# Four copies on one engine, a shorter distance at the last tiles, and a fifth output buffer in a two-layer expert kernel

## The chip, the cores and the metric

The kernel runs on one core of a Trainium2 chip. A core has a matrix engine (TensorE, PE in the profile; its weight loads are the row PEld), a vector engine (VectorE, DVE), an engine for activation functions (ScalarE, ACT), a general one (GpSimd, POOL) and one that mostly issues DMAs (SyncE, SP). Each works through its own queue in order; they wait for each other by semaphores. The time is the device time of one execution in microseconds, lower is better.

## The reference

The input x is 8 sequences of 256 tokens with 128 features, 2048 tokens in all, in float32. Two layers follow, each a conditioning step and a mixture of 8 experts (128 to 512 and back to 128).

```python
x = x + L0_ffn(L0_cond(x, itok_2))      # layer 0
x = x + L1_ffn(L1_cond(x, itok_8))      # layer 1

# L0_cond: scores = tanh(x W1 + b1) v; softmax over a prefix, a postfix or all other tokens; pooled x / count
# L0_ffn: gates = logits * (logits >= the 3072nd smallest logit); every expert for every token
h = gelu_tanh(x @ w1[e].T + b1[e]);  y = h @ w2[e].T + b2[e];  out = sum_e gates[e] * y
# L1_cond: a small adapter by the sequence's language, then a layer norm with that language's gamma and beta
# L1_ffn: layer norm; the two best of 8 experts for each token, weighted
out = sum over the two best of w * (gelu(xn @ w1[e] + b1[e]) @ w2[e] + b2[e]);  return out + residual
```

## The kernel before

**Front.** The 2048 tokens are four groups of 512 (`NG = 4`), each a tile of 128 partitions with four tokens in each. For each group TensorE turns the tokens into PSUM (L224, tile xTp), and a copy brings them to SBUF as xT: for groups 0 and 2 on ScalarE (L229), for groups 1 and 3 on VectorE (L227). `products` (L203) multiplies a group's xT with the conditioning weights and the gate's weights; a few matmuls into a tile `idle` (L190) only keep TensorE running. VectorE then adds a bias row bv (L206; bv itself is copied out of PSUM at L233), ScalarE takes tanh (L207), VectorE multiplies and sums (L211, L212). The sums of all groups are turned at once (L248); two scans over them (L251, L253), two more operations (L255, L256) and the matmuls `top` (L262) lead to the softmax and the pooling. The counts cnt (L314, L315) are needed only behind the pooling.

**Layer 0, dense.** `layer` goes over five units of tokens (three of 512, two of 256) and over 8 experts in each: four matmuls of 512 columns to the hidden layer (L784), its activation on ScalarE (L786), and four matmuls back (L764), one expert later. Between them a function `pump` takes single steps of what else is to do: a search for the threshold of the gates, the pooling of later groups, and for a finished unit the adapter, the norm, the routing and the scatter of its tokens to a list in DRAM, sorted by expert (xs, L676, from GpSimd).

**Layer 1, sparse.** The list is worked on in tiles of 128 rows of one expert. The first `SURE = 36` tiles (0 to 35) are always there. A tile k has four steps. `fetch` loads its rows (L814) and its expert's first weights (L822) by SyncE's queue. `turn` transposes the rows (L829), scales them on VectorE (L831) and copies the expert's bias (L833). `hidden` is four matmuls (L840) and four activations (L842). `output` is four matmuls (L849) into one of two PSUM buffers yps, an add of the expert's second bias on VectorE into a tile yt (L852, four buffers), a scale by the token's weight on ScalarE (L853), and a scatter of the 128 rows to their places in DRAM from GpSimd (ys, L854). A buffer of yt is free again when the scatter that reads it has landed.

The steps of several tiles are interleaved by three queues of the program: `fetched`, `flipped` (turned) and `hid` (with a hidden layer). `proceed(ahead, between)` does one `hidden` if more than `ahead` tiles are turned, and one `output` if more than `ahead` have a hidden layer. `AHEAD = 2` keeps two tiles' distance between the steps of one tile. After tile 35 is turned, `proceed(0)` empties the queues.

**End.** All engines then read the number of tiles (L901) and branch (L903) over a body for tiles 36 to 38, which these inputs don't need. Where it is left out, each engine brings the semaphores that the body would have raised up to date. Then the rows ys are loaded back (L911, two queues, eight tiles), added to the residual (L914, L915) and stored (L916).

The order of instructions on each engine is not the order of the lines alone: a planner of the language sets it from the dependences and its own estimates, so the built order has to be looked at where a change is made.

Of the kernel before, what the change touches and what calls it, by code (L numbers as in the profile page):

```python
# [10 lines left out]
F32 = mybir.dt.float32  # L11
# [10 lines left out]
B, S, D = 8, 256, 128  # L22
P = 128
# [19 lines left out]
SURE = 36  # L43
# [8 lines left out]
AHEAD = 2  # L52
# [16 lines left out]
def tile_adaln_ffn_d2(ctx: ExitStack, tc: tile.TileContext, x, ptype, lang, cols, b1v,  # L69
                      w10, w20, w11d, w21d, lw1, lw2, lgb, out):  # L70
    nc = tc.nc
# [6 lines left out]
    work = ctx.enter_context(tc.tile_pool(name="work", bufs=2))  # L78
# [27 lines left out]
    for e in range(E):  # L106
        t = first.tile([P, HC * P], F32, tag="w1", name=f"w10_{e}")
        nc.sync.dma_start(out=t, in_=w10[e])
        w10s.append(t)
        t = const.tile([P, HC, D], F32, name=f"w20_{e}")  # L110
# [42 lines left out]
    for b in range(B):  # L153
        at = nc.values_load(lgi[0:1, b:b + 1], engines=(SP,), min_val=0, max_val=NL - 1,
                            skip_runtime_bounds_check_because="a language's number")
        for lst, name, src, rows, width in (
# [3 lines left out]
            t = const.tile([rows, width], F32, name=f"{name}_{b}")  # L160
# [10 lines left out]
    xT, poolT, resid, gd0 = {}, {}, {}, {}  # L171
# [26 lines left out]
    def products(g):  # L198

        space = (psy, "y") if g < 2 else (psb, "big")  # L200
        xa = space[0].tile([P, GT, A + E], F32, tag=space[1], name=f"xa{g}")
        for t in range(GT):
            nc.tensor.matmul(xa[:, t, :], lhsT=xT[g][:, t * P:(t + 1) * P], rhs=col[:, C_W1:C_W1 + A + E],  # L203
                             start=True, stop=True)
        pass_time(1, ident, xT[g][:, :S])
        nc.vector.tensor_tensor(at[:, g], xa[:, :, :A], bv[:, 0].unsqueeze(1).to_broadcast([P, GT, A]), ALU.add)  # L206
        nc.scalar.activation(at[:, g], at[:, g], AF.Tanh)  # L207
        nc.scalar.copy(xg[g][:, :, D:D + E], xa[:, :, A:])

    def scores(g):  # L210
        nc.vector.tensor_tensor(at[:, g], at[:, g], bv[:, 1].unsqueeze(1).to_broadcast([P, GT, A]), ALU.mult)  # L211
        nc.vector.tensor_reduce(sl[:, g * GT:(g + 1) * GT], at[:, g], AX.X, ALU.add)  # L212
# [8 lines left out]
    for g in range(NG):  # L221
        tp = psb.tile([P, GT, P], F32, tag="big", name=f"xTp{g}")
        for t in range(GT):
            nc.tensor.transpose(tp[:, t, :], xg[g][:, t, :D], ident)  # L224
        xT[g] = keep.tile([P, GN], F32, tag="xT", name=f"xT{g}")
        if g % 2:
            nc.vector.tensor_copy(xT[g], tp.rearrange("p t d -> p (t d)"))  # L227
        else:
            nc.scalar.copy(xT[g], tp.rearrange("p t d -> p (t d)"))  # L229
        if not g:  # L230
            nc.tensor.matmul(bvp.rearrange("p c a -> p (c a)"), lhsT=ones[:A, :],
                             rhs=diag.rearrange("k c a -> k (c a)"), start=True, stop=True)
            nc.vector.tensor_copy(bv, bvp)  # L233
        else:
            products(g - 1)
        if g > 1:
            scores(g - 2)
# [21 lines left out]
    for g in range(NG):  # L259
        tp = psb.tile([P, 2, S], F32, tag="big", name=f"top{g}")  # L260
# [458 lines left out]
    def pump():  # L719
        if gd0:  # L720
            n = next(ready)
            if not n:
                gates0.append(gd0[0])
            if waiting and n >= 0 and n % DRAIN == 0:
                waiting.popleft()()
        if behind:
            if next(behind[0], done) is done:
                behind.popleft()
# [72 lines left out]
    def expert(k, *engines):  # L801

        rows, i = lists[listing(k)], k - SLOTS.get(listing(k) - 1, 0)
        return nc.values_load(rows[0:1, 1, i:i + 1], engines=engines, min_val=0, max_val=E - 1,
                              skip_runtime_bounds_check_because="at most E - 1, a sum of flags")
# [21 lines left out]
    def turn(k, xt, wt):  # L827
        tp = pss.tile([P, P], F32, tag="sm", name=f"xtp{k}")
        nc.tensor.transpose(tp, xt[:, :D], ident)  # L829
        xc = work.tile([P, P], F32, tag="xc", name=f"xc{k}", bufs=AHEAD + 3)  # L830
        nc.vector.tensor_scalar(xc, tp, col[:, C_LG:C_LG + 1], col[:, C_LB:C_LB + 1], ALU.mult, ALU.add)  # L831
        b1 = small.tile([P, HC], F32, tag="b1", name=f"b1_{k}", bufs=AHEAD + 3)
        nc.vector.tensor_copy(b1, b1all[:, bass.ds(expert(k, DVE), 1), :].rearrange("p o c -> p (o c)"))  # L833
        return k, xt, wt, xc, b1

    def hidden(k, xt, wt, xc, b1):
        hp = psb.tile([P, HC, P], F32, tag="big", name=f"hps{k}")
        hT = work.tile([P, HC, P], F32, tag="scr", name=f"hs{k}", bufs=NSCR)
        for c in range(HC):
            nc.tensor.matmul(hp[:, c, :], lhsT=wt[:, c * P:(c + 1) * P], rhs=xc, start=True, stop=True)  # L840
        for c in range(HC):
            nc.scalar.activation(hT[:, c, :], hp[:, c, :], AF.Gelu, bias=b1[:, c:c + 1])  # L842
        return k, xt, hT

    def output(k, xt, hT):
        ek = expert(k, PE, DVE)
        yp = psy.tile([P, D], F32, tag="y", name=f"yps{k}")
        for c in range(HC):
            nc.tensor.matmul(yp, lhsT=hT[:, c, :], rhs=w21[:, bass.ds(ek, 1), c * D:(c + 1) * D],  # L849
                             start=(c == 0), stop=(c == HC - 1))  # L850
        yt = work.tile([P, D], F32, tag="yt", name=f"yt{k}", bufs=4)
        nc.vector.tensor_tensor(yt, yp, b2all[:, bass.ds(ek, 1), :].rearrange("p o d -> p (o d)"), ALU.add)  # L852
        nc.scalar.activation(yt, yt, AF.Copy, scale=xt[:, D + 1:D + 2])  # L853
        move = nc.gpsimd.indirect_dma_start(  # L854
            out=ys, out_offset=bass.IndirectOffsetOnAxis(ap=xt.bitcast(I32)[:, D:D + 1], axis=0),
            in_=yt, in_offset=None, bounds_check=2 * NT * P - 1, oob_is_err=False)
        tc.declare_no_dep(move.ins, group="outputs", reason="no two outputs share a row")
        tc.add_to_no_dep_group("outputs", move.ins)

    fetched, flipped, hid = deque(), deque(), deque()  # L860

    def proceed(ahead, between=lambda: None):
        if len(flipped) > ahead:
            hid.append(hidden(*flipped.popleft()))
        between()
        if len(hid) > ahead:
            output(*hid.popleft())

    def ahead(k):

        if k < SURE:
            finished(("first", listing(k)))
            fetched.append(fetch(k))
# [14 lines left out]
    for k in range(PRIMED, SURE):  # L888
        ahead(k + LEAD)
        if k == SLOTS[NU - 2]:  # L890

            while len(flipped) > 1 or len(hid) > 1:
                proceed(1)
        flipped.append(turn(*fetched.popleft()))
        pump()
        proceed(AHEAD, pump)
    while flipped or hid:
        proceed(0)
    while behind:
# [3 lines left out]
    with tc.If(more > SURE - SLOTS[NU - 2]):  # L903
        for k in range(SURE, NSLOT):
            output(*hidden(*turn(*fetch(k))))
# [61 lines left out]
```

## Time and profile before

| | us |
|---|---|
| three runs | 380.01, 388.47, 388.97 (median 388.47) |
| the profiled execution, and its span | 380.68, 379.0 |
| TensorE busy | 345.8 (91% of the span) |
| VectorE, ScalarE, GpSimd busy | 195.0, 167.0, 94.5 |
| mean clock granted to TensorE | 0.977 of full |
| first matmul of layer 0 | starts at 29.37 |
| add of tile 35 (L852) | starts at 361.64 |
| last scatter ys (L854) | starts at 362.64 |
| first reload yg (L911) | issued at 365.17 |

All rows from the third on come from the trace of the profiled execution; times within it count from the start of its span. A line of the page's groups names the line of the kernel, the engine, the operation, what is written and read, how often, and the busy time. In a timeline a row has its start, its duration, and in brackets how long the engine had been idle and what ended that. An engine's name with a q is its sequencer, which waits, branches and issues DMAs. The ends of matmuls are modelled.

### The profile page before, as it was taken

The numbers are of one execution on the slowest core, as the hardware profiler recorded it, in microseconds if no ns is written. First come the engines' busy times: TensorE is split into PE (matmuls) and PEld (weight loads), VectorE is DVE, ScalarE is ACT, GpSimd is POOL, SyncE is SP. The second block draws the span as 40 slices with busy tenths as digits, with TensorE's granted clock in tenths as the row PEclk, the third lists the DMA queues.
The fourth block names the chain that finished last, engine by engine and source line by source line (L and its number), as shares of the span: only waits on it lengthen the run. The fifth ranks groups of instructions, "written<-read, shape, count | busy, mean of one in ns | idle before, by whom it ended". The sixth has DMA issues, their size and how long they took to land. (4 is left out here: it accounts for less than half of the span.)

```text
span 379.0 us, 5911 instructions
## 1 busy us (share of the span) xinstructions
PE 345.8 (91%) x1596; PEld 233.0 (61%) x1596; DVE 195.0 (51%) x801; ACT 167.0 (44%) x387; POOL 94.5 (25%) x142
## 2 busy tenths in 40 slices
PE   6799999999999999999999999989989879999900
PEld 6695444444444445445445688857869769999900
DVE  4775565542245675565512474847576644333305
ACT  2166434553542244223443244425635637567800
POOL 8100000000000030650350021262045565444530
PEclk9999999999999999999999999999999998999975
DMA  6935999005222101210130001126543554566136
GB/s 189 382 84 150 368 379 356 4 0 148 69 77 102 56 30 55 63 49 30 56 69 14 28 29 42 36 65 175 151 121 107 162 162 121 168 187 173 47 117 244
DMA packets 33603, 46.12 MB, mean 122 GB/s; under 512 B 5349, under 2 KB 16375, under 8 KB 33569
## 3 DMA queue, kind: packets, MB, share of 16 engines
q1 hardware_dynamic: 29024, 39.26, 34.6%
q0 software_dynamic: 2304, 4.37, 3.2%
q10 hardware_dynamic: 2240, 2.10, 1.6%
q8 instruction: 14, 0.23, 0.3%
q14 instruction: 21, 0.16, 0.1%
HBM read 31.57 MB, written 14.39 MB: 121 GB/s over the span
## 5 line engine op out<-in xcount | busy, mean ns | idle before, releaser
L786 ACT ACTIVATE hT_first<-hp_first,col 128x512 f32<-128x512 f32 (+1 forms) x160 | 93.4, 601 | 103.3 <-PE hp_first L784 102.3
L784 PE MATMUL hp_first<-poolT,w 128*128 128x512 f32 (+1 forms) x320 | 121.2, 513 | 1.3 <-DVE xr L591 0.7
L764 PE MATMUL yp_first<-hT_first,w 128*128 128x512 f32 (+1 forms) x320 | 120.6, 511 | 0.0
L784 PEld LDWEIGHTS hp_first<-poolT,w 128*128 128x128 f32 x320 | 58.8, 190 | 44.2 <-issue 38.2
L764 PEld LDWEIGHTS yp_first<-hT_first,w 128*128 128x128 f32 x320 | 59.0, 190 | 42.5 <-issue 38.6
L676 POOL DMA_INDIRECT xs<-zr,pos x32 | 31.5, 986 | 64.3 <-DVE pos L674 27.9
L842 ACT ACTIVATE hs<-hps,b 128x128 f32<-128x128 f32 x144 | 40.6, 365 | 11.2 <-PE hps L840 5.3
L854 POOL DMA_INDIRECT ys<-yt,xt x36 | 35.2, 977 | 40.9 <-ACT hs L842 28.3
L849 PE MATMUL yps<-w,hs 128*128 x288 | 39.6, 283 | 2.5 <-DVE row L558 2.4
L840 PE MATMUL hps<-xc,wt 128*128 128x128 f32 x288 | 39.2, 280 | 1.1 <-issue 1.1
L849 PEld LDWEIGHTS yps<-w,hs 128*128 128x128 f32 x288 | 35.7, 195 | 4.3 <-issue 3.5
L752 DVE SCALAR_TENSOR_TENSOR part_first<-yp_first,col,gbc_first 128x512 f32<-128x512 f32 (+1 forms) x28 | 17.2, 614 | 40.4 <-PE yp_first L764 39.9
L840 PEld LDWEIGHTS hps<-xc,wt 128*128 128x128 f32 x288 | 36.0, 196 | 0.8 <-issue 0.6
L853 ACT ACTIVATE yt<-yt,xt 128x128 f32<-128x128 f32 x36 | 14.6, 405 | 23.3 <-issue 15.0
L754 DVE TENSOR_TENSOR acc_first<-acc_first,part_first 128x512 f32<-128x512 f32 (+1 forms) x35 | 20.1, 580 | 0.5
L579 POOL MEMSET ha<- 1x512 f32 x5 | 2.6, 516 | 67.6 <-PE dp L588 67.4
L406 POOL DMA_DIRECT2D gd_L<-gT_L x1 | 0.6, 649 | 74.3 <-DVE gT_L L404 74.3
L833 DVE COPY b<-col 128x4 f32 x36 | 7.2, 200 | 23.0 <-ACT hs L842 17.7
L852 DVE TENSOR_TENSOR yt<-yps,b2all 128x128 f32<-128x128 f32 x36 | 10.5, 291 | 14.8 <-PE yps L849 7.1
L831 DVE TENSOR_SCALAR xc<-xtp,col 128x128 f32<-128x128 f32 x36 | 14.4, 401 | 4.0 <-PE xtp L829 2.4
L772 ACT ACTIVATE y_first<-yp_first,col 128x512 f32<-128x512 f32 x8 | 5.5, 687 | 24.2 <-PE yp_first L764 24.2
L420 DVE TENSOR_SCALAR_CACHE_REDUCE fl<-logit,tr 128x128 f32<-128x128 f32 x46 | 13.5, 343 | 0.6
(205 smaller groups left out, 304.2 us busy)
## 6 DMA issues: line engine op xcount, KB each, us to landing
wt<-in_w_dram SPq DMA_DIRECT2D x36, 256.0 KB
xs<-empty SPq DMA_DIRECT2D x1, 8580.0 KB
w<-in_w_dram SPq DMA_DIRECT2D x24, 256.0 KB
gbc_first<-gd_L SPq DMA_DIRECT2D x24, 256.0 KB
xt<-xs SPq DMA_DIRECT2D x36, 65.0 KB
gbc_first<-gd_L SPq DMA_DIRECT2D x16, 128.0 KB
lgb<-in_lgb_dram SPq DMA_DIRECT2D x8, 128.0 KB
yg<-ys ACTq DMA_DIRECT2D x4, 256.0 KB
```

The source lines that it names most:

```text
L676: move = nc.gpsimd.indirect_dma_start(out=xs, out_offset=bass.IndirectOffsetOnAxis(ap=pos[:, t:t + 1], axis=0), in_=zr[s][:, t, :], in_off ...
L752: nc.vector.scalar_tensor_tensor(part, y, bias, gbc, ALU.add, ALU.mult)
L754: nc.vector.tensor_tensor(accs[u], accs[u], part, ALU.add)
L764: nc.tensor.matmul(yp, lhsT=w2s[e][:, c, :], rhs=hT[:, c, :], start=(c == 0), stop=(c == HC - 1))
L784: nc.tensor.matmul(hp, lhsT=w1s[e][:, c * P:(c + 1) * P], rhs=sources[g][:, o * P:o * P + n], start=True, stop=True)
L786: nc.scalar.activation(hT[:, c, :], hp, act, bias=col[:, cb1 + e * HC + c:cb1 + e * HC + c + 1])
L831: nc.vector.tensor_scalar(xc, tp, col[:, C_LG:C_LG + 1], col[:, C_LB:C_LB + 1], ALU.mult, ALU.add)
L840: nc.tensor.matmul(hp[:, c, :], lhsT=wt[:, c * P:(c + 1) * P], rhs=xc, start=True, stop=True)
L842: nc.scalar.activation(hT[:, c, :], hp[:, c, :], AF.Gelu, bias=b1[:, c:c + 1])
L849: nc.tensor.matmul(yp, lhsT=hT[:, c, :], rhs=w21[:, bass.ds(ek, 1), c * D:(c + 1) * D], start=(c == 0), stop=(c == HC - 1))
L853: nc.scalar.activation(yt, yt, AF.Copy, scale=xt[:, D + 1:D + 2])
L854: move = nc.gpsimd.indirect_dma_start(out=ys, out_offset=bass.IndirectOffsetOnAxis(ap=xt.bitcast(I32)[:, D:D + 1], axis=0), in_=yt, in_off ...
```

## The change

Three edits. The copies of the transposed tokens of all four groups go to ScalarE. The output tile yt has five buffers in place of four. And for the last three of the 36 tiles (k = 33, 34, 35) `proceed` is called with a distance of 1, then outputs are taken until at most two tiles (for k = 35 at most one) stand with a hidden layer and no output.

```diff
         xT[g] = keep.tile([P, GN], F32, tag="xT", name=f"xT{g}")
-        if g % 2:
-            nc.vector.tensor_copy(xT[g], tp.rearrange("p t d -> p (t d)"))
-        else:
-            nc.scalar.copy(xT[g], tp.rearrange("p t d -> p (t d)"))
+        nc.scalar.copy(xT[g], tp.rearrange("p t d -> p (t d)"))
...
-        yt = work.tile([P, D], F32, tag="yt", name=f"yt{k}", bufs=4)
+        yt = work.tile([P, D], F32, tag="yt", name=f"yt{k}", bufs=5)
...
         flipped.append(turn(*fetched.popleft()))
         pump()
-        proceed(AHEAD, pump)
+        if k < SURE - 3:
+            proceed(AHEAD, pump)
+        else:
+
+            proceed(1, pump)
+            while len(hid) > (1 if k == SURE - 1 else 2):
+                output(*hid.popleft())
     while flipped or hid:
         proceed(0)
```

In the built order of the changed kernel the matmuls of `output` for tile 32 stand ahead of those of `hidden` for tile 34, and those of `output` for tile 33 ahead of those of `hidden` for tile 35; on ScalarE the scale of tile 32 stands ahead of the activations of tile 34. Besides, the scale of tile 35 on ScalarE and its scatter on GpSimd stand behind the branch, no longer ahead of it, and the four operations on cnt on VectorE stand around the last sum (L212), ahead of the first scan (L251).

## The prediction

> **What bounds the kernel now.** I read the page first, then the timeline of the first 16 us, then the last 30 us engine by engine, and last the instructions of the lines that the change moves. The profiled execution took 380.68 us, of which 379.0 us are span. In the page I look at the busy shares and at the chain that ended last:
>
> ```profile
> span 379.0 us, 5911 instructions
> PE 345.8 (91%) x1596; PEld 233.0 (61%) x1596; DVE 195.0 (51%) x801; ACT 167.0 (44%) x387; POOL 94.5 (25%) x142
> ...
> PE   6799999999999999999999999989989879999900
> ...
> PE yps L849 3%; PE hps L840 3%; DMA yg<-ys 2%; ACT hs L842 1%; DMA ys<-yt,xt 1%; POOL ys L854 1%; DVE o L914 0%; PE xtp L829 0%; DVE o L915 0%; SPq L911 0%; ACT yt L853 0%; DVEq L963 0%; DVE yt L852 0%; POOLq L901 0%; POOLq L854 0%
> ```
>
> The row of tenths says that TensorE is full from slice 3 to about slice 37. What is won before slice 3 is therefore passed on one for one, and what is won or lost after slice 37 adds directly to the end. Between them the change moves nothing. So there are two stages to price. The first is the front, in the timeline (start, duration, engine, line; in brackets the idle time before and who ended it):
>
> ```profile
> 6.01 0.58 ACT L229 COPY xT<-xTp 128x512 f32<-128x512 f32 x1 [1.25 <-PE xTp L224]
> ...
> 7.92 0.58 ACT L229 COPY xT<-xTp 128x512 f32<-128x512 f32 x1 [1.32 <-PE xTp L224]
> ...
> 8.97 0.68 PE L190 MATMUL idle<-xT,ident 128*128 128x256 f32 x2
> ...
> 9.36 0.20 DVE L233 COPY bv<-bvp 128x64 f32<-128x64 f32 x1
> ...
> 9.76 1.26 DVE L227 COPY xT<-xTp 128x512 f32<-128x512 f32 x2
> ...
> 10.48 1.08 PE L203 MATMUL xa<-col,xT 128*128 128x40 f32 x8 [0.84 <-DVE xT L227]
> ```
>
> The two DVE copies are ready to run at 7.6 and 8.4 (their transposes are done) but stand in DVE's queue behind small work on flags until 9.76, and TensorE waits 0.84 us for the first. ScalarE is idle then.
>
> The second stage is the end. The last scatters of output rows on GpSimd, and what comes behind them:
>
> ```profile
> 358.64 0.97 POOL L854 DMA_INDIRECT ys<-yt,xt  x1 [0.35 <-ACT hs L842]
> 359.96 0.97 POOL L854 DMA_INDIRECT ys<-yt,xt  x1 [0.35 <-issue]
> 361.24 0.97 POOL L854 DMA_INDIRECT ys<-yt,xt  x1 [0.30 <-issue]
> 362.64 0.97 POOL L854 DMA_INDIRECT ys<-yt,xt  x1 [0.44 <-issue]
> ```
>
> They follow each other every 1.31 us, GpSimd's own pace. The chain goes on from the last one: 2.46 us until it has landed, then 6.65 us of reloading. The instructions of the branch (L901 the loading of its count, L903 the branch; nanoseconds, then when):
>
> ```profile
> L901 POOLq TENSOR_LOAD <-total x1: 581/581/581, 362.4 to 362.4; - x1
> ...
> L903 POOLq COMPARE_BRANCH x1: 45/45/45, 363.1 to 363.1; - x1
> ...
> L903 POOLq INC_SWDGE_SEM x1: 1620/1620/1620, 363.3 to 363.3; - x1
> ...
> L852 DVEq EVENT_SEMAPHORE x32: 21/21/21, 293.4 to 359.9; - x32
> ```
>
> The third line is the one to remember: after the untaken body GpSimd spends 1.62 us raising the semaphores of the body's three scatters. Today that lies behind the last scatter, beside its landing. The fourth line is DVE's check, before each add, that its output buffer is free again: all 32 took 21 ns.
>
> **What the Trainium skill says.** "Perfetto Trace Analysis", Optimizing Scalar/DVE Operations: some operations can go to either engine, and the fixed cost on PSUM is smaller on Scalar. The trace agrees: 585 ns on ScalarE, 668 ns on DVE. "DMA: Bandwidth & Descriptors", Anatomy of one DMA: about 2.0 us are fixed, most of it the receipt of the write; the chain's 2.46 us agrees. "Advanced Engine Details and Errata", Control Flow Timing: a compare-and-branch is about 108 ns; here it was 45 to 72 ns on DVE, ScalarE and GpSimd. No page prices the step that took 1.62 us.
>
> **The change part by part.**
>
> *Copies to ScalarE.* Two copies of 0.668 us leave DVE, two of 0.585 us come to ScalarE, which is idle from 8.5 to 11.26. Done in turn from 7.5, they end by 9.2. The next thing late for the second group's products is then TensorE's filler (8.97 + 0.68 = 9.65, its last matmul issued at 9.27) and the PSUM buffer that the copy of bv frees at 9.56. They start near 9.6 instead of 10.48, and each later group follows by TensorE's own 1.32 us: gain 0.86 us. In the built order DVE's four ops on cnt (0.21, 0.19, 0.21, 0.23 us) move ahead of the scan. The first falls between the last product and the last sum, and costs at most 0.1; the other three lie beside the two transposes that the scan waits for anyway, and one leaves the gap between L255 and L256. Net gain 0.8 us (0.7 to 0.9), with TensorE full behind it. On SP one small store passes one weight load; both are needed 200 us later, so nothing.
>
> *Fifth output buffer.* The 32 checks at 21 ns say that four never ran out: 0.
>
> *Distance.* In the built order of TensorE one thing differs: the output of tile 32 goes ahead of the hidden layer of tile 34, and the output of 33 ahead of that of 35. The matmul sum is the same. On ScalarE the scale of tile 32 (0.31 us net) now stands ahead of tile 34's activation. What could be won is an earlier scatter 32, but scatters are paced by GpSimd from 357.33 on, five in a row; that start is set by tile 31's add, which DVE began at 356.28 although TensorE's row ended tile 31 at 354.33 by the chain. The wait named is TensorE's, so its signal came about 1.9 us late. If that repeats, the gain is 0. If it does not, scatter 31 can go at 355.87 (354.56 plus 1.31), and 34 follows its own matmuls.
>
> *What moves with it.* In the built order tile 35's scale on ScalarE and its scatter on GpSimd now stand after the branch, no longer before it. Ahead of the last scatter GpSimd therefore does, in turn: load 0.58, branch and check about 0.35, semaphore step 1.62. Queued behind it is only that scatter, but the reload on both queues waits for its landing. On ScalarE load and branch (0.48 and some 0.3) end before tile 35's add: 0. For the step there are two bounds. At the kernel's start the same operation took 27 ns; if it is as cheap here, the 0.93 us of load and branch hides under the 1.31 us pace: 0. If it takes 1.62 as in the row, and like there ends 1.35 us after the scatter ahead of it (362.21 to 363.56 in today's times), the last scatter starts near 363.85 in place of 362.64: +1.2. A gain below nothing is excluded, since the scatter only gets more ahead of it. I take 1.2, because the row was measured in the same place.
>
> Sum against the execution's own 380.68: -0.8 + 0 + 0 + 1.2 = +0.4, so 381.1. The three runs shown are 380.01, 388.47 and 388.97: two groups, 2.2% apart, and the profile belongs to the lower. I carry the +0.4 to the median: **388.9**.
>
> **The rivals.**
> - *Signals on time.* Scatter 34 starts at 359.75 and the last at 359.75 + 2.6 = 362.35, 0.3 before today's: -0.8 - 0.3 = -1.1, so 387.4. For it: the lateness shows on few tiles only. Against: it hangs on TensorE's place in its stream, which hardly moves.
> - *The step is free* (nothing to wait for): -0.8, so 387.7. For it the 27 ns, against it the 1.62.
> - *ScalarE's queue turns the order against us: slower.* If tile 31's signal comes later than about 354.5, its scale and tile 32's hold up tile 34's activation by 0.35, tile 33's output waits for tile 31's PSUM buffer with nothing put in between, and TensorE ends at 360.2 in place of 359.97. The last two tiles' signals trail as today (add 35 at 361.64), so 0.2 to 0.9 more: -0.8 + 1.2 + 0.9 = +1.3, so 389.8.
> - *The change is as worked out, but the median falls in the lower group*: 380.01 plus 0.4 is 380.4, 380.68 plus 0.4 is 381.1; with -1.1, 378.9 to 379.6.
>
> **How the numbers follow.** About 2% is what a measurement of this kernel can tell from no change. Chances: forecast 0.36, signals on time 0.14, step free 0.12, slower by ScalarE's queue 0.11, lower group 0.22, and 0.05 that the kernel before, measured beside it, lies low while this one lies high. The first four are all within 2%: 0.73. The lower group reads as faster by over 2% below 380.7, which I give four fifths of it: 0.18, and 0.04 to the middle. The last reads as slower: 0.05. The likeliest case alone spans 388.2 to 389.8 (the copies' and the step's bounds). The range must take in the lower group, since without it more than 2 in 10 would be left out: 379.0 to 390.0.
>
> **What would show it.** Right, if the second group's products start near 9.6 and hp's first matmul near 28.6 (now 29.37); if no add waits for a buffer; if on GpSimd the semaphore step lies between the last two scatters, now 2.4 to 2.7 us apart where they were 1.40. Wrong, if those two stay under 1.5 us apart (the step is free), if the adds follow their matmuls at once at the end, or if the front's gain is lost again before 250 us.

## The result and the profile after

The changed kernel took 384.44 us in the median of eleven runs (381.83 to 390.46), the kernel before, run beside it, 386.38 us in the median of eleven (380.01 to 389.14). Both medians mix two groups of executions that lie 2% apart (of those profiled below, the slower ones are the five in which TensorE's clock became full only after 22 us), so the comparison is made with the ratio of the faster group alone: 1.0088, with a 95% interval of 1.0061 to 1.0115. The change costs 0.9%, some 3.4 us of 382. That lies within the 2% that the forecast called no change, and it is more than the forecast's +0.4 us.

The profiled execution took 384.38 us, with a span of 382.7 (before: 380.68 and 379.0). From its page, the busy shares, TensorE's row of tenths and the last steps of the chain that ended last:

```profile
span 382.7 us, 5910 instructions
PE 347.7 (91%) x1596; PEld 234.8 (61%) x1596; DVE 193.5 (51%) x799; ACT 168.5 (44%) x389; POOL 94.7 (25%) x142
...
PE   5999999999999999999999999999989869999700
...
DMA ys<-yt,xt 4%; DMA yg<-ys 2%; DVE o L917 0%; DVE o L918 0%; SPq L914 0%; DVE yt L849 0%; DVEq L966 0%; POOLq L966 0%; DVE xc L828 0%; POOLq L906 0%; DVEq L801 0%; DVE b L830 0%; POOLq L851 0%; ACT hs L839 0%; DVEq L917 0%
```

The first slice has dropped from 6 to 5, and slice 38, TensorE's last, from 9 to 7: TensorE is idle for longer at both ends. The row `ys<-yt,xt` has grown from 1% to 4% of the chain, but it should not be read as longer landings. Followed in time, the chain has two such entries: 2.21 us from the last scatter to its landing, and 13.02 us from a scatter at 352.87 to 365.89, within GpSimd's semaphore step. That scatter had landed by 354.98; its semaphore counted up once more at 365.89, in the step, so the chain took the step for a landing.

Timeline of the front (start, duration, engine, line, what is done, in brackets the idle time before and who ended it):

```profile
6.99 0.39 DVE L216 TENSOR_TENSOR diag<-ident,bva 32x64 f32<-32x64 f32 x1 [4.42 <-DMA bva<-in_b1v_dram]
...
8.11 2.82 PE L224 MATMUL xTp<-ident,xg 128*128 128x128 f32 x12
...
9.26 0.59 ACT L226 COPY xT<-xTp 128x512 f32<-128x512 f32 x1 [2.65 <-PE xTp L224]
...
10.11 0.59 ACT L226 COPY xT<-xTp 128x512 f32<-128x512 f32 x1 [0.27 <-PE xTp L224]
...
12.48 0.98 PE L203 MATMUL xa<-col,xT 128*128 128x40 f32 x8
```

The copies are where the diff puts them, but everything is late. The twelve transposes took 2.82 us where they took 1.53 before, and the second group's products start at 12.48. The trace says why. Its record of the granted clock begins, with the full clock, at 11.62 us, where it began at 6.43 in the profile of before. In both profiles TensorE's matmuls of one size start every 0.21 us ahead of that entry and every 0.11 us behind it, so it ran at half its speed until then. (The record is empty there, and the views show a full clock.) The first matmul of layer 0 starts at 31.27 (before 29.37).

Timeline of the end, the scatters on GpSimd and the add of tile 34; then, from the instructions of the branch, GpSimd's semaphore step (nanoseconds, then when):

```profile
359.65 0.97 POOL L851 DMA_INDIRECT ys<-yt,xt  x1 [0.31 <-ACT hs L839]
...
360.93 0.97 POOL L851 DMA_INDIRECT ys<-yt,xt  x1 [0.30 <-issue]
362.76 0.29 DVE L849 TENSOR_TENSOR yt<-yps,b2all 128x128 f32<-128x128 f32 x1 [3.54 <-PE yps L846]
...
363.76 0.97 POOL L851 DMA_INDIRECT ys<-yt,xt  x1 [1.86 <-DVE yt L849]
...
366.86 0.97 POOL L851 DMA_INDIRECT ys<-yt,xt  x1 [2.13 <-DMA ys<-yt,xt]
```

```profile
L906 POOLq COMPARE_BRANCH  x1: 45/45/45, 364.1 to 364.1; - x1
...
L906 POOLq INC_SWDGE_SEM  x1: 1613/1613/1613, 364.4 to 364.4; - x1
```

Two things are late here. The scatter of tile 34 waits for an add that itself waits 3.54 us for TensorE, 2.83 us behind the scatter before it where it was 1.28. And the last scatter comes 3.10 us after that, where it was 1.40, with the 1.61 us of the semaphore step in between. (Its bracket names a landing of `ys`; that is again the step, as the runs below show.)

To compare executions with different starts, I use one length throughout: the **tail**, from the first hidden matmul of tile 28 to the start of the last scatter. It was 342.19 to 362.64 = 20.45 us before and 343.13 to 366.86 = 23.73 after, +3.28. Of these, 1.58 lie ahead of tile 34's scatter and 1.70 between it and the last one. The span's +3.7 is then: 0.94 ahead of tile 28, 3.28 in the tail, and -0.51 between the last scatter and the end, where the profile of before was long (16.31 us; 15.0 to 16.0 in all others).

The front had lost 1.90 us. On TensorE this stays 1.90 until 236 us, is 1.28 at 253, 1.77 at 329 and 0.94 at tile 28. From layer 0's first matmul to tile 28 the ten profiles with trailing results (explained in the next section) took between 311.8 and 313.7 us. So a gain or loss in the front is passed on in full to 236 us, and beyond that a single profile shows it to no better than 1 to 2 us. Within these ten the five with the fifth buffer lie low (311.8 to 312.7, the others 312.6 to 313.7). About half of that stands before the first output tile, where the buffer is not yet used, and on the other chip it is not seen; whether it is chance stays open.

### The profile page after: what moved, and what is told of

It reads as the page before. It is cut to its first block, busy times and chain, and to the rows that moved or that the text cites. A ratio compares the mean times of both kernels' runs of the same rounds, so it can differ in the third digit from the quotient of the medians.

```text
span 382.7 us, 5910 instructions
## 1 busy us (share of the span) xinstructions
PE 347.7 (91%) x1596; PEld 234.8 (61%) x1596; DVE 193.5 (51%) x799; ACT 168.5 (44%) x389; POOL 94.7 (25%) x142
```

## The experiments

Theory A: the tail costs the time, by the semaphore step ahead of the last scatter and by a new order that makes TensorE's late results hurt; the late clock in the front is chance. Rival B: the copies on ScalarE made the front late. Four kernels ran on one chip, eight on another. The first compares whole times and tails where TensorE's results are on time (each add of the last seven tiles follows its matmuls by 0.04 us); on the second chip they trail by up to 2 us, as in the first comparison. All ratios are to the kernel before, run beside them.

| kernel | chip | full clock from | layer 0 from | tail | last two scatters | ratio, 95% interval |
|---|---|---|---|---|---|---|
| before | first comparison | 6.43 | 29.37 | 20.45 | 1.40 | |
| after | first comparison | 11.62 | 31.27 | 23.73 | 3.10 | 1.0088 [1.0061, 1.0115] |
| e_copies | on time | 10.39 | 30.17 | 18.59 | 1.27 | 0.9977 [0.9942, 1.0012] |
| e_bufs | on time | 24.96 | 35.88 | 20.05 | 2.73 | 1.0031 [0.9991, 1.0071] |
| e_distance | on time | 10.81 | 30.33 | 18.21 | 1.27 | 0.9991 [0.9955, 1.0027] |
| e_copdist | on time | 10.90 | 30.62 | 18.21 | 1.27 | 0.9989 [0.9954, 1.0023] |
| after_again | trailing | 22.65 | 34.57 | 23.71 | 3.11 | 1.0167 [1.0072, 1.0262] |
| repair | trailing | 25.38 | 36.25 | 21.89 | 1.28 | 1.0007 [0.9975, 1.0039] |
| copies_buf | trailing | 5.88 | 28.53 | 21.57 | 2.44 | 0.9985 [0.9947, 1.0022] |
| one_body | trailing | 5.94 | 28.61 | 23.62 | 3.02 | 1.0055 [1.0018, 1.0092] |
| bufs_only | trailing | 11.46 | 30.93 | 21.57 | 2.44 | 0.9989 [0.9955, 1.0022] |
| copies_only | trailing | 25.41 | 36.29 | 20.68 | 1.52 | 0.9979 [0.9940, 1.0018] |
| distance_only | trailing | 10.97 | 30.51 | 21.87 | 1.28 | 0.9998 [0.9961, 1.0036] |
| dist_psum | trailing | 24.84 | 35.80 | 20.66 | 1.58 | 1.0005 [0.9967, 1.0043] |

A whole time is uncertain by some 0.35%, that is 1.3 us: enough to see the whole change, not one part of it. The tails repeat better: 23.73 and 23.71, 21.87 and 21.89, 21.57 and 21.57 for pairs of profiles with the same end, though 20.45 and 20.68 for the kernel before and the copies alone. So the parts are read from the tails, each from one or two profiles, and good to about 0.2 us. The kernel before itself was profiled in the first comparison only; a tail that is set against 20.45 is set against that one.

### The fifth buffer alone

```diff
-        yt = work.tile([P, D], F32, tag="yt", name=f"yt{k}", bufs=4)
+        yt = work.tile([P, D], F32, tag="yt", name=f"yt{k}", bufs=5)
```

> The kernel before with the fifth output buffer and nothing else. In the built order this moves one instruction: tile 35's scatter on GpSimd stands behind the branch, no longer ahead of it. Theory A (the slowdown is the semaphore step of the branch ahead of the last scatter): the last two scatters are 2.7 to 3.1 us apart instead of 1.40, and the kernel is 1.3 to 1.7 us slower than before. Theory B (the copies made it slower): no change. The prediction's own step, taken alone, said 0 for the buffer and +1.2 for the branch, without seeing that they are one.

> The fifth buffer alone, once more. I count from the start of tile 28's hidden matmuls to the last scatter, so that the front and the clock's start drop out. Where TensorE's signals trail at the end (kernel before: 20.4 us), theory A expects 21.5, last two scatters 2.4 apart; where they are on time, 1.4 to 1.5 more than the copies alone (11.2 to 11.3 after tile 34's matmuls there).

On the first chip the last two scatters were 2.73 us apart, 1.46 more than in the three kernels beside it. On the second they were 2.44 apart and the tail 21.57, 1.12 more than before. The traces show what was expected. The expected 1.3 to 1.7 us of the whole time did not show: +0.3% and -0.1%, both intervals hold 1, and the second ends at +0.22%, 0.84 us, below even the tail's 1.12. Part of that is the long end in the profile of before: from tile 28 to the end of the span the buffer alone takes 37.51 us, the kernel before 36.77 and the copies alone 36.42, so 0.7 to 1.1 us more. GpSimd's scatters and its semaphore step in the kernel with the fifth buffer alone, on the second chip:

```profile
360.58 0.97 POOL L854 DMA_INDIRECT ys<-yt,xt  x1 [0.35 <-issue]
361.85 0.97 POOL L854 DMA_INDIRECT ys<-yt,xt  x1 [0.30 <-issue]
...
364.29 0.97 POOL L854 DMA_INDIRECT ys<-yt,xt  x1 [1.47 <-issue]
```

```profile
L903 POOLq INC_SWDGE_SEM  x1: 1613/1613/1613, 361.8 to 361.8; - x1
```

The add of tile 35 was done here by 362.64 and its scale by 363.07; still the scatter waits until 364.29. In the built order this kernel differs from the one before by one instruction: tile 35's scatter, which stands behind the branch. The step ends at 363.43 and the scatter starts 0.87 us later, as it does in every profile with this order (359.06 after 358.19 on the first chip, 366.86 after 365.99 in the changed kernel). So the buffer is not idle at all. It never serves to avoid a wait, but it changes what the planner does at the branch; why the planner does so is not on record.

### The copies alone

```diff
-        if g % 2:
-            nc.vector.tensor_copy(xT[g], tp.rearrange("p t d -> p (t d)"))
-        else:
-            nc.scalar.copy(xT[g], tp.rearrange("p t d -> p (t d)"))
+        nc.scalar.copy(xT[g], tp.rearrange("p t d -> p (t d)"))
```

> The kernel before with all four copies on ScalarE and nothing else. Theory A and the prediction: the second group's products start at 9.6 instead of 10.48 where TensorE's clock is full as early as before, and the kernel is 0.8 us faster; the late full clock in the changed kernel's profile was chance. Theory B: TensorE's full clock comes late again (11.6 instead of 6.4), hp's first matmul is 1.9 us later, and the kernel is 1 to 2 us slower.

> The copies alone, once more. From tile 28's hidden matmuls to the last scatter the time of the kernel before. Where TensorE's clock is full by 6.5 us, hp's first matmul is at 28.5 to 28.6 (29.37 before); where it comes at 10 us or later, no gain from the copies. In all 0 to 0.8 us faster than the kernel before.

0.9977 and 0.9979: a sign of 0.8 us, not a proof, and no sign of a loss. Rival B falls. The full clock came late in the profiles of both, but the table shows that this has nothing to do with the copies: the kernels with the front of before had it from 6.43, 10.81, 10.97, 11.46, 24.84 and 24.96. What the copies do where the clock comes early is seen in the kernel with copies and fifth buffer (below), front timeline:

```profile
6.36 0.21 DVE L216 TENSOR_TENSOR diag<-ident,bva 32x64 f32<-32x64 f32 x1 [3.80 <-DMA bva<-in_b1v_dram]
...
7.05 1.53 PE L224 MATMUL xTp<-ident,xg 128*128 128x128 f32 x12
...
7.74 1.56 ACT L226 COPY xT<-xTp 128x512 f32<-128x512 f32 x3 [1.15 <-PE xTp L224]
...
9.23 0.68 PE L190 MATMUL idle<-xT,ident 128*128 128x256 f32 x2
...
9.74 0.98 PE L203 MATMUL xa<-col,xT 128*128 128x40 f32 x8
...
28.53 1.12 PE L781 MATMUL hp_first<-poolT,w 128*128 128x512 f32 x2
```

The second group's products start at 9.74 (10.48 before), with no wait ahead of them, and layer 0 at 28.53 (29.37 before): 0.84 us gained. The clock, full at 5.88 instead of 6.43, is not the reason: the first group's products started later than before (8.41 against 8.15). one_body, the other kernel with an early clock, has 28.61. Where the clock comes at 10.4 to 11.6, layer 0 starts 19.65 to 19.78 us after it with the copies on ScalarE and 19.47 to 19.54 without: nothing is gained. There the copies wait for TensorE, whose twelve transposes take 2.82 us instead of 1.53, and in the kernel with the distance alone (clock from 10.81) TensorE no longer waits for VectorE's copy.

### The distance alone

```diff
-        proceed(AHEAD, pump)
+        if k < SURE - 3:
+            proceed(AHEAD, pump)
+        else:
+
+            proceed(1, pump)
+            while len(hid) > (1 if k == SURE - 1 else 2):
+                output(*hid.popleft())
```

> The kernel before with the changed distance over the last three tiles and nothing else. In the built order TensorE has the outputs of tiles 32 and 33 ahead of the hidden layers of 34 and 35, ScalarE has tile 32's scale ahead of tile 34's activation; GpSimd is as before. Theory A: TensorE waits for tile 31's buffer and its last signals trail, so the last scatter comes 0.5 to 1.5 us later, with the last two still 1.3 to 1.5 us apart. Prediction: 0, scatters stay 1.31 us apart from tile 31 on. Theory B: 0.

> The changed distance alone, once more. From tile 28's hidden matmuls to the last scatter: where TensorE's signals trail, 21.9 us (before: 20.4), so the kernel 1.4 us slower than before; where they are on time, 0.4 us less than before. The last two scatters 1.3 us apart in both.

Where TensorE's results are on time the tail is 18.21 in place of 18.59: a gain of 0.38, since the last three outputs are spread so that tile 34's scatter no longer queues behind 33's. Where they trail, the tail is 21.87, 1.42 more than before. The whole time (0.9998) misses the expected +1.4 us, though its upper bound of +0.36% just reaches it. TensorE, VectorE and GpSimd at that place, of this kernel:

```profile
357.34 0.29 DVE L852 TENSOR_TENSOR yt<-yps,b2all 128x128 f32<-128x128 f32 x1 [3.29 <-PE hps L840]
...
357.78 1.13 PE L849 MATMUL yps<-w,hs 128*128 x8 [0.70 <-DVE yt L852]
...
358.74 1.06 PE L840 MATMUL hps<-xc,wt 128*128 128x128 f32 x8
...
360.88 1.26 PE L849 MATMUL yps<-w,hs 128*128 x8 [0.19 <-issue]
...
362.73 0.29 DVE L852 TENSOR_TENSOR yt<-yps,b2all 128x128 f32<-128x128 f32 x1 [3.50 <-PE yps L849]
...
363.73 0.97 POOL L854 DMA_INDIRECT ys<-yt,xt  x1 [1.81 <-ACT yt L853]
...
365.01 0.97 POOL L854 DMA_INDIRECT ys<-yt,xt  x1 [0.30 <-issue]
```

The first row is the add of tile 31, late; it frees one of two PSUM buffers. Tile 33's output waits 0.70 us for it, and only then comes tile 35's hidden layer, then its activation, then its output. Before, the hidden layers of 34 and 35 stood ahead of these waits.

The last three rows show how this reaches the end. The add at 362.73 is tile 34's, 19.59 us after tile 28's start. In the kernel before it stood at 17.21:

```profile
359.40 0.29 DVE L852 TENSOR_TENSOR yt<-yps,b2all 128x128 f32<-128x128 f32 x1 [1.17 <-PE yps L849]
```

These 2.38 us are 0.82 by which TensorE's records of tile 34's output end later, and 1.56 by which the add trails them more (2.04 us instead of 0.48). GpSimd has sent tile 33's scatter off by then and stands idle for 1.81 us, and the last scatter follows tile 34's at GpSimd's pace. Tile 35's own add is only 0.71 us later than before and no longer sets the end.

### The distance with more PSUM buffers

```diff
-        yp = psy.tile([P, D], F32, tag="y", name=f"yps{k}")
+        space, tag = (psb, "big") if SURE - 3 <= k < SURE else (psy, "y")
+        yp = space.tile([P, D], F32, tag=tag, name=f"yps{k}")
```

> The changed distance alone, with the outputs of tiles 33, 34 and 35 in the other PSUM pool (four buffers in place of two), in the same built order. Theory A1 (tile 33's output waits for tile 31's PSUM buffer, which its late add frees): where signals trail, 0.7 to 1.4 us less than the distance alone from tile 28's matmuls to the last scatter. Theory A2 (TensorE is behind its records there, so that its waits in the records are not idle time): no difference.

The tail is 20.66, 1.21 less than with the distance alone: within what A1 expected, and nearly the tail of before. From the timeline:

```profile
362.55 1.06 PE L850 MATMUL yps<-w,hs 128*128 x8
...
362.99 0.29 DVE L853 TENSOR_TENSOR yt<-yps,b2all 128x128 f32<-128x128 f32 x1 [3.31 <-PE yps L850]
...
363.44 1.06 PE L840 MATMUL hps<-xc,wt 128*128 128x128 f32 x8
...
365.89 0.29 DVE L853 TENSOR_TENSOR yt<-yps,b2all 128x128 f32<-128x128 f32 x1 [1.46 <-PE yps L850]
```

Tile 33's output now starts ahead of tile 31's late add, and tile 35's hidden layer 14.65 us after tile 28's in place of 15.60. Tile 34's add (the last row) is back at 17.10 us after tile 28's start, 0.04 behind its matmuls. So the cost of the distance hangs on the PSUM buffers of these tiles. Three tiles got other buffers, but in the trace only tile 33 had waited for one. Why tile 34's add trails its matmuls by 2 us with the wait and by 0.04 without it is not shown.

### The changed kernel again, and with four buffers

```diff
-        yt = work.tile([P, D], F32, tag="yt", name=f"yt{k}", bufs=5)
+        yt = work.tile([P, D], F32, tag="yt", name=f"yt{k}", bufs=4)
```

> The changed kernel with four output buffers again: copies on ScalarE and changed distance. Tile 35's scatter and its scale stand ahead of the branch again. Theory A: 1.3 to 1.7 us faster than the changed kernel, that is 0 to +1 against the kernel before. Theory B: as slow as the changed kernel, +3.

> The changed kernel as it is, beside the next three. Theory A (the fifth buffer's move of the last scatter behind the branch is the one cost): last two scatters 2.7 to 3.1 us apart, +1 to +3 us against the kernel before. Rival (the first comparison's +0.9% was that chip's late signals of TensorE at the end, and the branch costs nothing by itself): where TensorE's signals follow its matmuls at once, no difference.

> The changed kernel with four output buffers, once more, on the same chip as the changed kernel. Theory A: 1.3 to 1.7 us faster than the changed kernel, last two scatters 1.27 to 1.4 us apart. Rival: the same time as the changed kernel.

With four buffers the loss is gone from the whole time (0.9989 and 1.0007). In the tail it is 1.82 us on the second chip (23.71 to 21.89), somewhat above the expected 1.3 to 1.7. The ratio of the changed kernel itself, 1.0167, can't be taken at face value: five of its six executions took 388.48 to 390.94 us, the profiled one of them with the clock late (22.65), and they are set against executions of the kernel before of 379 to 383 us. Its tail is the one of the first comparison.

### Copies and fifth buffer, without the distance

```diff
-        if k < SURE - 3:
-            proceed(AHEAD, pump)
-        else:
-
-            proceed(1, pump)
-            while len(hid) > (1 if k == SURE - 1 else 2):
-                output(*hid.popleft())
+        proceed(AHEAD, pump)
```

> The changed kernel without the changed distance: copies and fifth buffer. Tile 35's scatter is behind the branch, its scale ahead of it. Theory A: last two scatters 2.7 us apart, the time of the changed kernel or up to 0.4 us more, since the distance brought the last scatter 0.38 us nearer to TensorE's end where signals are on time; where they trail as in the first profile of the changed kernel, 0.5 to 1.5 us less than the changed kernel.

The tail is 2.14 us shorter than the changed kernel's (21.57 against 23.71), more than the 0.5 to 1.5 expected, and the last two scatters are 2.44 apart, less than the 2.7 expected; the whole time is that of before. The tail shows that the parts do not add: the buffer alone costs 1.12, the distance alone 1.42, together 3.28. The missing 0.74 us, above what the tails are uncertain by, is in the profiles, for the most part between the last two scatters. With the buffer alone, tile 34's scatter queues behind 33's, and meanwhile GpSimd's queue has already loaded the count and branched; the semaphore step starts with the scatter (361.81 and 361.85). With the distance too, nothing is queued, since tile 34's scatter waits for its add: loading and branch end after the scatter has started, and the step starts at 364.38, 0.62 after the scatter's 363.76.

### A smaller body of the branch

```diff
-        for k in range(SURE, NSLOT):
+        for k in range(SURE, SURE + 1):
             output(*hidden(*turn(*fetch(k))))
```

> The changed kernel with one tile in the branch's body instead of three (the body is not taken; for other inputs this leaves out the work of two tiles). Tile 35's scatter is still behind the branch. If the semaphore step's 1.62 us is paid per scatter of the body: 0.54 us, the last two scatters 1.6 to 2.0 us apart, and the kernel about 1.1 us faster than the changed one. If it waits for the scatter ahead of it or is a fixed price: 1.62 us again, and no difference.

The semaphore step takes 1.607 us with one scatter in the body, 1.613 with three: a fixed price. It doesn't wait for the scatter ahead either. In the kernel with the fifth buffer on the first chip it ended at 358.19, while that scatter's landing was signalled from 358.38 to 359.29; the last scatter itself started at 359.06, so it did not wait for this landing. No run took the step away and left the scatter behind the branch, so its share of the cost is read from the timelines. From the profile of the smaller body:

```profile
L906 POOLq INC_SWDGE_SEM  x1: 1607/1607/1607, 362.4 to 362.4; - x1
```

Its ratio, 1.0055, is +2.1 us (0.7 to 3.5). Tail +3.17 and front -0.76 make +2.4.

## Why the prediction was right and wrong

**Copies.** The step held in size and place where its condition held: it said products near 9.6 and layer 0 near 28.6, measured are 9.74 and 28.53 or 28.61. What failed is that it took the clock of one profile for granted. Of fourteen profiled executions three had the full clock by 6.5 us; with a later one the gain is nothing. On record it is therefore between 0 and -0.8, and the +1.90 us in the profile of after is the clock, not the change. "Passed on one for one" holds to 236 us; from there on the executions differ by more than the gain. Of the two kernels with the early clock, one_body was 0.76 us ahead of the kernel before at 235 us, level with it at 253 and 0.69 ahead again at 271.

**Fifth output buffer.** The checks still took 21 ns, as said, so no wait went. But "0" was wrong: the step that was priced under "What moves with it" belongs to the buffer, and exists without the other two parts. The diff's least edit carries one of its two costs.

**What moves with it.** Right in kind: the semaphore step lies between the last two scatters and takes 1.61 us. The size was right for the buffer alone (1.2 put, 1.12 measured on the chip with trailing results, 1.46 on the other), and too small for the change: 3.10 - 1.40 = 1.70 in the profiles, 1.82 against the kernel with four buffers; the two scatters are 3.10 apart where 2.4 to 2.7 was the sign. The working let the step end 2.32 us after the start of the scatter ahead, and the last scatter start 0.29 us behind the step. In the changed kernel these are 2.23 and 0.87, so the term that was too small is the stretch between step and scatter, 0.87 us in every profile with this order. With the buffer alone they are 1.57 and 0.87: the queue has a backlog there, which hides the load and the branch, and this cancels the other error. That 1.2 fitted the buffer alone is luck.

**Distance.** This is the step that failed. It put 0, with the argument that GpSimd's pace of 1.31 us hides everything from tile 31 on. The pace hides only while scatters are queued, and behind tile 33's the queue ran empty: with the distance alone GpSimd stood idle for 1.81 us until tile 34's scatter, and the last scatter came 1.42 later than before. The rival "ScalarE's queue turns the order against us" had the start of the mechanism: tile 33's output waits for tile 31's PSUM buffer with nothing put in between. It stood at 0.11, and its size was 0.23 us on TensorE and at most 0.9 in all. Measured with the distance alone, the end of tile 35's output on TensorE moved from 17.77 to 19.00 us after tile 28's start, 1.23 later. The working moved the wait but not what stands behind it: hidden layer, activation and output of tile 35. Nor had it that tile 34's result would come 2.38 us later and set the end in place of tile 35's. That ScalarE's queue caused it is not shown; that it hangs on the PSUM buffers is, since other buffers took 1.21 of the 1.42 away.

**The other rivals.** "Signals on time" describes the chip where they are: there the distance by itself gains 0.38, where 0.3 was put. "The step is free" fell in every profile with the scatter behind the branch.

**Sum.** Put: -0.8 + 0 + 0 + 1.2 = +0.4. By the tails: 0 to -0.8 for the copies and +3.28 for the end, +2.5 to +3.3, against the measured +2.3 to +4.4 us of the ratio. The forecast of no change by 2% held because the errors were small beside 2%, not because each step was right. The forecast time of 388.9 rested on a median of three runs, two of them from the slower group; with eleven that median was 2 us lower. The measured 384.44 lies inside 379.0 to 390.0, a range that took in both groups of executions and so says little about the steps.

## What to carry to other kernels

Look where the last instructions stand relative to a branch that is not taken, on every engine, and check it for each edit alone: a buffer count that no wait depends on moved a scatter behind a 1.6 us step here. When a step is moved at the end of a pipeline, follow the chain behind the wait (buffer, hidden layer, activation, output, scatter), since nothing comes after it to cover it, and a price that was read beside a full queue can be too low once the queue is empty. And read a front's gain from several profiles, because the start of the full clock may decide whether it exists.

The kernel with the copies alone is the only one with both ratios below 1, 0.9977 and 0.9979, and each interval holds 1: no version was shown to beat the kernel before.

## What was not expected of the hardware

- The start of TensorE's full clock varies between executions of the same front: 5.9 to 6.4 us in three profiles, 10.4 to 11.6 in six, 22.7 to 25.4 in five (one of these had it for 3.4 us from 5.58 and lost it again). Layer 0 starts 28.5 to 29.4, 30.2 to 31.3 and 34.6 to 36.3 us into the span accordingly. In both profiles of the changed kernel the small table bva was used late (VectorE's diag at 6.99; 6.10 to 6.67 elsewhere), which left TensorE idle for 1.5 to 1.7 us; whether that delayed the clock was not tried.
- In the first comparison and on the chip of the later eight kernels, TensorE's results at the end came as much as 2.1 us after the records' end of the matmuls (tile 34's add in the changed kernel 2.09 after it), on the other chip 0.04 us. The two differ earlier too: at tile 13 the activation starts 6.4 to 6.7 us after the first of its matmuls where results trail, 1.6 to 1.7 where they don't, and only the former show a stretch of 3.4 to 6.8 us at half clock between 313 and 326 us (one of them another at 260). What stops TensorE there stays open.
- The semaphore step of the untaken branch on GpSimd takes 1.61 to 1.64 us in all fourteen profiles, for one as for three scatters in the body, and in the two profiles with the fifth buffer alone it ended before the scatter ahead of it had landed (358.19 against 358.38 to 359.29, 363.43 against 363.92 to 364.09).
